# A four-layer convolution network: columns of the last 3x3 convolution transformed too for three of six rows, its result added to the output by an accumulating DMA, squares on ScalarE

## The chip, the cores and the metric

The kernel runs on one core of a Trainium2 chip. The metric is the device time of one execution in microseconds. The kernel before was run three times: median 2744.98 us, lowest 2739.24, highest 2749.27. One more execution was recorded by the hardware profiler; its own time is 2735.2 us and its span, from the first recorded instruction to the last, 2733.4 us.

Names of engines: TensorE (PE, with PEld for its weight loads), VectorE (DVE), ScalarE (ACT), GpSimd (POOL) and SyncE (SP). In this kernel SP issues most loads, ScalarE some stores, and GpSimd some loads and stores.

## The reference, cut to what matters

The input x is [4, 256, 64, 64] in float32. Four layers each add a function of the group norm of x to x:

```
def _gn(v, G=32, eps=1e-5):          # mean and variance over 8 channels x 64 x 64
    ...
    return ((g - m) / jnp.sqrt(s + eps)).reshape(v.shape)

x = x + _L0_conv_ref(_gn(x), ...)    # axial attention along rows, three batch norms
x = x + _L1_conv_ref(_gn(x), ...)    # 3x3 convolution with ternary weights
x = x + _L2_conv_ref(_gn(x), ...)    # two grouped 3x3 convolutions of signs, three batch norms
x = x + _L3_conv_ref(_gn(x), ...)    # 3x3 convolution with generated weights
```

The last layer's 256 x 256 x 3 x 3 weights are generated from a 64 x 64 x 3 x 3 tensor and sixteen pairs (a, b), and the convolution is an ordinary one with a border of zeros and a bias:

```
act = w * a / (1.0 + jnp.exp(w * b))
W = act.transpose(0, 2, 1, 3, 4, 5).reshape(R0 * OOC, R1 * OIC, K1, K2)
out = jax.lax.conv_general_dilated(x, W, window_strides=(1, 1), padding=[(1, 1), (1, 1)], ...)
return out + bias[None, :, None, None]
```

## The kernel before, in words

**The whole.** The layers run one after the other. Between them tensors lie in DRAM scratch: the second layer's sum in x2_d, the third layer's two result parts in z_d and y_d (y_d before its batch norm), the last layer's transformed weights in u3_d. The last layer's input is built when it is read: x2 plus z times a scale per channel, and for the first of two channel tiles also y times sy2.

**The generated weights.** During the first layer's scoring loop, weight_steps (L598) is a generator: each step of the loop calls next(weights) once (L652), so a bit of weight work on VectorE is put between the attention's operations. weights_3(t, dx) makes the six transformed weight rows of one input tile t and one column tap dx and GpSimd's queue stores them; weights_2 follows for the third layer.

**The last convolution.** Channels are two tiles of 128 partitions, t for input and co for output. An image b is cut into halves h of 32 rows. A chunk (b, h, co) is 128 output channels of half an image; there are sixteen. The convolution is a Winograd F(4,3) along rows only: from each group of six input rows, input_rows (L1036) forms six transformed rows k, with 12 VectorE operations of 128x528 for a half of one tile; output_rows (L1055) multiplies each k with its weights and combines six products to four output rows. Columns are handled directly with three taps dx. So a chunk takes 6 rows x 3 taps x 2 input tiles = 36 matmuls of 512 columns (8 row groups by 64) in f32, and every f32 matmul stands in the trace as two records. Products go to a ring of seven PSUM tiles. The combination is one ScalarE copy for each of two products (L1084), 10 VectorE operations (L1086 to L1099), and 4 more (L1101) that add the result to the residual, which is still in SBUF in the half-image buffer xs. GpSimd then stores that half image (finish_3, L1760, sixteen stores of 1 MB).

**Loading an image.** load_3 (L1724) is called for a tile t: SP loads the two halves of x2 (1 MB each) and then z and y in parts of 256 KB through four small buffers; VectorE adds z (L1736) and, for t = 0, y (L1743, L1746). Statistics for the group norm are bn_stats on VectorE (L1114), except for tile 0 of image 0, where the sum comes with the addition (accum_out) and the squares are summed on ScalarE (L1749). norm combines the partitions with small matmuls (L115, L125, L126), and transform has ScalarE write the normalised half into a padded buffer (L1182, L1186) before input_rows.

**The order.** conv_layer (L1120) returns functions, called at L1762 to L1779. rest() writes chunk (b, 0, 0), then the load of the next image's tile 0, chunk (b, 0, 1), the load of tile 1 and its norm, chunk (b, 1, 0), the transforms of the next image's first half, chunk (b, 1, 1), and those of its second half. A scheduler then fixes each engine's order from this text; parts under tc.high_priority are put as early as their data allow. In the order before, image 0's tile 1 is loaded, normalised and transformed under high priority between the last chunks of the third layer. Its first chunk multiplies with tile 1 first (order (1, 0)), since tile 0 needs y_d, which is stored last. Every engine's own queue is in order: an instruction that waits holds those behind it.

**Buffers.** Six half-image buffers x0 to x5 rotate by X_PLACES over the four images, six transformed buffers t0 to t5 over the half images. The small load buffers come in two pairs. The two weight buffers u0 and u1 are loaded by GpSimd's queue (six loads of 768 KB) during the third layer.

Of the kernel before, what the change touches and what calls it, by code (L numbers as in the profile page):

```python
# [41 lines left out]
def network(ctx: ExitStack, tc, x, wqkv, relm, relt, relw, relv, counts, masks, vecs, rowv, ab, w1, l2w1, l2w2, l3w, mats, out):  # L42
# [25 lines left out]
    u3_d = scratch("u3_d", [P, 2, 3, 6, C])  # L68
    bk_d = [dram.tile([P, 2, 3, 4 * 3 * 64], BF16, name=f"bk_d{i}", tag=f"bk_d{i}") for i in range(2)]
# [340 lines left out]
    with ExitStack() as ph:  # L410
# [157 lines left out]

        def weights_2(i, g):
# [28 lines left out]
        def weight_steps():  # L598
            for t in range(2):
                for dx in range(3):  # L600
                    yield from weights_3(t, dx)
                    yield
            for i in range(2):
                for g in range(2):
                    yield from weights_2(i, g)
                    yield
# [137 lines left out]
    def from_scores(general, keep):  # L744
# [291 lines left out]
        def input_rows(v, pad, pinned):  # L1036

            d = [pad[:, r : r + 29 : 4, :] for r in range(6)]
            stt = nc.vector.scalar_tensor_tensor
            start = stt(v[:, 5], d[2], -4.0, d[4], ALU.mult, ALU.add)  # L1040
            if pinned:
                tc.keep_in_program_order(start)
            stt(v[:, 0], d[1], -4.0, d[3], ALU.mult, ALU.add)
            nc.vector.tensor_tensor(v[:, 1], v[:, 5], v[:, 0], ALU.add)  # L1044
            nc.vector.tensor_tensor(v[:, 2], v[:, 5], v[:, 0], ALU.subtract)
            nc.vector.tensor_tensor(v[:, 5], d[4], d[2], ALU.subtract)
            nc.vector.tensor_tensor(v[:, 0], d[3], d[1], ALU.subtract)
            stt(v[:, 3], v[:, 0], 2.0, v[:, 5], ALU.mult, ALU.add)
            stt(v[:, 4], v[:, 0], -2.0, v[:, 5], ALU.mult, ALU.add)
            stt(v[:, 0], d[0], 4.0, d[4], ALU.mult, ALU.add)  # L1050
            stt(v[:, 0], d[2], -5.0, v[:, 0], ALU.mult, ALU.add)
            stt(v[:, 5], d[1], 4.0, d[5], ALU.mult, ALU.add)
            stt(v[:, 5], d[3], -5.0, v[:, 5], ALU.mult, ALU.add)

        def output_rows(ring, taken, op, u, vs, co, xh, bias, name, order):  # L1055


            ms = [None] * 6
            c, sm = [None, None], [None, None]

            def product(k, t, first, last):
                if first:
                    ms[k] = ring[taken[0] % len(ring)].tile([P, 8, 64], F32, name=f"{name}_{k}", tag="conv")
                    taken[0] += 1
                for dx in range(3):
                    nc.tensor.matmul(  # L1066
                        ms[k], lhsT=u[t][:, dx, k, bass.ts(co, P)], rhs=vs[t][:, k, :, dx : dx + 64],
                        start=(first and dx == 0), stop=(last and dx == 2),
                    )

            if order:
                for k in range(6):
                    product(k, order[0], True, False)
            for k in range(6):
                if order:
                    product(k, order[1], False, True)
                else:
                    product(k, 0, True, False)
                    product(k, 1, False, True)
                if k in (2, 4):  # L1080
                    i = k // 2 - 1
                    c[i] = op.tile([P, 8, 64], F32, name=f"{name}_c{i}", tag=f"c{i}", bufs=1)
                    sm[i] = op.tile([P, 8, 64], F32, name=f"{name}_s{i}", tag=f"s{i}", bufs=1)
                    nc.scalar.copy(c[i], ms[k])  # L1084
                    if i == 0:
                        nc.vector.scalar_tensor_tensor(sm[i], ms[1], bias, c[i], ALU.add, ALU.add)  # L1086
                        nc.vector.scalar_tensor_tensor(c[i], ms[1], bias, c[i], ALU.add, ALU.subtract)
                    else:
                        nc.vector.tensor_tensor(sm[i], ms[3], c[i], ALU.add)
                        nc.vector.tensor_tensor(c[i], ms[3], c[i], ALU.subtract)  # L1090
            x4 = xh.rearrange("p (q r w) -> p q r w", r=4, w=64)
            (d12, d34), (s12, s34) = c, sm
            o = [op.tile([P, 8, 64], F32, name=f"{name}_o{r}", tag="o", bufs=1 if general else 2) for r in range(4)]
            nc.vector.tensor_tensor(o[0], ms[0], s12, ALU.add)
            nc.vector.tensor_tensor(o[0], o[0], s34, ALU.add)
            nc.vector.scalar_tensor_tensor(o[1], d34, 2.0, d12, ALU.mult, ALU.add)
            nc.vector.scalar_tensor_tensor(o[2], s34, 4.0, s12, ALU.mult, ALU.add)
            nc.vector.scalar_tensor_tensor(o[3], d34, 8.0, d12, ALU.mult, ALU.add)
            nc.vector.tensor_tensor(o[3], ms[5], o[3], ALU.add)  # L1099
            for r in range(4):  # L1100
                nc.vector.tensor_tensor(x4[:, :, r, :], x4[:, :, r, :], o[r], ALU.add)  # L1101
# [16 lines left out]
        X_PLACES = [(0, 1, 2, 3), (4, 5, 0, 2), (1, 3, 4, 0), (5, 2, 1, 4)]  # L1118

# [777 lines left out]
```

## Time and profile before

| | |
|---|---|
| median of three runs | 2744.98 us |
| the profiled execution, and its span | 2735.2 us, 2733.4 us |
| TensorE busy over the span | 88% |
| VectorE busy over the span | 72% |
| ScalarE busy over the span | 44% |
| last VectorE operation of the third layer's last chunk | about 2193 us |
| first and last matmul of the last convolution | 2192.34 us, 2720.6 us |
| output stores of 1 MB, issue to landing | 4.1 us median |

The profile gives all times in microseconds from the start of the span. A group is named by its line, engine, operation and tiles; its mean is the duration of one instruction, and the idle time is that of its engine just ahead of it, with what ended it. Consecutive VectorE operations overlap a little, so the distance from start to start is shorter than the duration. TensorE's granted clock (PEclk) is given as a share of full speed.

### The profile page before, as it was taken

The page shows a single profiled execution, that of the slowest core. Times are in us where ns is not written, and L with a number is a line of the kernel's source. Part 1 is how long each engine was busy: PE and PEld are TensorE (multiplying, and loading weights), DVE is VectorE, ACT ScalarE, POOL GpSimd, SP SyncE. Part 2 cuts the span into 40 slices and gives each one's busy share as a digit, 9 for nine tenths or more (in the row PEclk, how much of TensorE's full clock was granted, in tenths as well). Part 3 has the DMA queues.
Part 4 walks back from the last instruction along what each step waited for, and adds up shares of the span by engine and source line. Part 5 has one row for each costly group of instructions (what it writes and reads, how often), then busy time and mean ns, then how long its engine had stood idle before and what let it go on. Part 6 is the DMA issues. An engine that isn't in the chain of part 4 may idle for free.

```text
span 2733.4 us, 78106 instructions
## 1 busy us (share of the span) xinstructions
PE 2393.6 (88%) x34632; PEld 1574.3 (58%) x34632; DVE 1978.0 (72%) x3372; ACT 1202.9 (44%) x1984; POOL 105.2 (4%) x201
## 2 busy tenths in 40 slices
PE   7999788889998788888784999998979859999998
PEld 4666555556666566666663777775545424444443
DVE  6665788888675466666567989887888877867742
ACT  3555245555555644454444656553458411110100
POOL 0000100000001000000000000000000000000000
PEclk9999899999999799989986999999989979999999
DMA  6866366667666877777777556424347742424110
GB/s 237 270 199 194 97 182 183 164 169 189 154 150 150 257 258 251 264 241 256 249 240 265 196 173 201 155 101 155 120 157 255 280 155 92 154 93 139 47 45 33
DMA packets 287996, 489.86 MB, mean 179 GB/s; under 512 B 32737, under 2 KB 149089, under 8 KB 274849
## 3 DMA queue, kind: packets, MB, share of 16 engines
q1 hardware_dynamic: 224992, 359.52, 43.3%
q0 software_dynamic: 14400, 66.53, 6.3%
q10 hardware_dynamic: 48256, 58.73, 6.2%
q8 instruction: 273, 4.47, 0.7%
q14 instruction: 75, 0.61, 0.1%
HBM read 281.46 MB, written 203.23 MB: 177 GB/s over the span
## 4 chain that ended last, share of the span: by engine, by line
issue 36%; PE 34%; DVE 13%; DMA 9%; ACT 5%; SPq 2%; POOL 1%; DVEq 0%; POOLq 0%; ACTq 0%
PE dc L1353 10%; PE pd L505 5%; PE po L293 3%; PE pv L308 3%; DMA at_d<-o_False 3%; PE pq L526 3%; PE e_False L867 2%; DMA x<-x_d 2%; DVE pt L877 2%; PE pa_False L945 1%; PE den_False L918 1%; PE pr_False L936 1%; PE pe_False L970 1%; DMA qc_False<-q_d 1%; DVE e_tr L1446 1%
## 5 line engine op out<-in xcount | busy, mean ns | idle before, releaser
L1066 PE MATMUL gc<-gtr,g_u 128*128 128x512 f32 x1152 | 505.3, 601 | 13.3 <-DVE gtr L1044 6.7
L1066 PEld LDWEIGHTS gc<-gtr,g_u 128*128 128x128 f32 x1152 | 219.9, 192 | 289.9 <-issue 271.2
L512 DVE STREAM_TRANSPOSE t<-pd 128x1024 f32<-128x1024 f32 x256 | 304.4, 1228 | 92.3 <-PE pd L505 87.0
L505 PE MATMUL pd<-rm,qb 64*32 64x256 f32 x8192 | 306.1, 389 | 41.4 <-DVE t L512 33.3
L1457 PE MATMUL pc<-e_tr,e_k 128*64 128x512 bf16 x2304 | 265.2, 391 | 20.3 <-DVE e_tr L1446 13.9
L532 ACT ACTIVATE o<-pq 128x512 f32<-128x512 f32 x256 | 150.4, 593 | 267.2 <-PE pq L526 258.4
L1353 PE MATMUL dc<-dh,d_u 128*128 128x512 f32 x768 | 229.7, 410 | 22.5 <-ACT dh L1330 21.4
L505 PEld LDWEIGHTS pd<-rm,qb 64*32 64x32 f32 x8192 | 169.8, 108 | 133.3 <-DVE t L512 58.8
L907 ACT ACTIVATE pt<-pt,sm 128x512 f32<-128x512 f32 x256 | 162.5, 709 | 174.6 <-DVE pt L877 156.4
L1353 PE MATMUL dc<-dl,d_u 128*128 128x512 f32 x768 | 226.6, 405 | 1.9 <-DVE dl L1331 1.8
L1457 PEld LDWEIGHTS <-e_k 128*64 128x64 bf16 x2304 | 147.4, 112 | 135.1 <-issue 28.7
L526 PEld LDWEIGHTS pq<-t,t 64*64 64x64 f32 x8192 | 144.7, 137 | 88.6 <-issue 71.3
L526 PE MATMUL pq<-t,t 64*64 64x64 f32 x8192 | 166.6, 225 | 31.5 <-issue 26.1
L1353 PEld LDWEIGHTS dc<-dh,d_u 128*128 128x128 f32 x768 | 146.3, 192 | 63.4 <-ACT dh L1330 22.9
L877 DVE TENSOR_TENSOR pt<-e_False,si_False 128x1024 f32<-128x1024 f32 x128 | 151.5, 1215 | 31.9 <-PE e_False L867 26.8
L1084 ACT COPY gc_c<-gc 128x512 f32<-128x512 f32 x32 | 18.6, 580 | 345.5 <-PE gc L1066 345.5
L1353 PEld LDWEIGHTS dc<-dl,d_u 128*128 128x128 f32 x768 | 144.8, 190 | 43.2 <-DVE dl L1331 4.7
L867 PE MATMUL e_False<-qc_False,rw 32*128 32x256 f32 x1024 | 130.7, 476 | 26.5 <-DVE pt L877 13.6
L538 ACT ACTIVATE sq<-o 128x1024 bf16<-128x1024 f32 x128 | 135.3, 1057 | 4.0
L293 PE MATMUL po<-xg,wt 128*128 128x512 f32 x256 | 122.3, 618 | 5.9 <-DVE st L300 4.3
L970 PE MATMUL pe_False<-pt,ve 128*32 128x64 f32 x4096 | 92.6, 246 | 38.2 <-issue 30.7
L308 PE MATMUL pv<-wt,xg 128*128 128x256 f32 x512 | 120.2, 383 | 0.0
(401 smaller groups left out, 3594.6 us busy)
## 6 DMA issues: line engine op xcount, KB each, us to landing
si_False<-qk_d SPq DMA_DIRECT2D x64, 1024.0 KB
qk_d<-o SPq DMA_DIRECT2D x496, 128.0 KB
x<-x_d SPq DMA_DIRECT2D x32, 1056.0 KB
xa<-in_x SPq DMA_DIRECT2D x16, 1024.0 KB
vt_d<-vs ACTq DMA_DIRECT2D x32, 512.0 KB
q_d<-qs SPq DMA_DIRECT2D x64, 256.0 KB
qb<-q_d SPq DMA_DIRECT2D x128, 128.0 KB
qc_False<-q_d SPq DMA_DIRECT2D x64, 256.0 KB
```

The source lines that it names most:

```text
L293: nc.tensor.matmul(psf, lhsT=wt[:, t, bass.ts(o, P)], rhs=xg[:, t, :], start=(t == 0), stop=(t == 1))
L308: nc.tensor.matmul(pv[:, j, :], lhsT=xg[:, t, pix], rhs=wt[:, t, C : 2 * C], start=(t == 0), stop=(t == 1),)
L505: nc.tensor.matmul(pds[t][32 * c : 32 * c + 32, m].rearrange("p j k -> p (j k)"), lhsT=q[rows, 2 * (gp % 2) + g, a, 32 * nb : 32 * nb + 32 ...
L512: nc.vector.transpose(ts[t][:, :, 32 * jh : 32 * jh + 32].rearrange("p a j b -> p j a b"), pds[t].rearrange("p m j k -> p j m k"),)
L526: nc.tensor.matmul(ps[nb][64 * g : 64 * g + 64, m, :], lhsT=ts[1][rows, n // 2, :, n % 2], rhs=ts[0][rows, n // 2, :, n % 2], start=True, ...
L532: nc.scalar.activation(o[:, :, n : n + 8, :], ps[nb].rearrange("p n (a b) -> p a n b", b=2), AF.Copy, accum_out=acc[:, nb, gp, col : col + 1],
L867: nc.tensor.matmul(es[x_ // 2][:, x_ % 2, :, :, par], lhsT=rw[rows, 63 - i : 127 - i].rearrange("p j r -> p (j r)"), rhs=q[rows, :, par, k ...
L877: nc.vector.tensor_tensor(dst, e, src, ALU.add)
L907: nc.scalar.activation(s, s, AF.Exp, scale=s2q[:, gp : gp + 1])
L1066: nc.tensor.matmul(ms[k], lhsT=u[t][:, dx, k, bass.ts(co, P)], rhs=vs[t][:, k, :, dx : dx + 64], start=(first and dx == 0), stop=(last and ...
L1353: nc.tensor.matmul(at[k], lhsT=u[t][:, dx, k, bass.ts(co, P)], rhs=v[:, k, :, dx : dx + 64], start=(first and p_ == 0 and dx == 0), stop=( ...
L1457: nc.tensor.matmul(m[64 * g : 64 * g + 64], lhsT=parts[:, g, i, k, dx, :], rhs=vs[g][:, k, 8 * (q % 2) : 8 * (q % 2) + 8, dx : dx + 64], s ...
```

## The change

Of the six transformed rows, k = 0, 2 and 4 are now transformed along columns as well, by a Winograd F(2,3): two output columns from four input columns with four products instead of six. input_rows writes these three rows to a scratch tile (gtm), and a new function input_columns makes four column terms c from it, with four VectorE operations of 768 elements. The rows k = 1, 3, 5 keep the three taps. Weights for the column terms 1 and 2 are prepared by a new part of the weight generator, weights_c, and stored in uc_d; terms 0 and 3 use u3_d with dx = 0 and dx = 2.

output_rows now has nine products per chunk: for each even k two that hold two column terms of 256 columns each (terms 1 and 2, terms 0 and 3), for each odd k one of 512. That is 24 matmuls of 256 columns and 18 of 512. columns and whole combine a pair: two ScalarE operations of 256 and two VectorE operations of 512 for an even row. The result goes to one tile of four rows, o4, with a single buffer.

The residual is no longer added in SBUF for 14 of the 16 chunks. load_3 has ScalarE's queue store the built half image to out as soon as it is complete, and the chunk's result is added onto it by a DMA with accum_op on GpSimd's queue. The last two chunks (b = 3, h = 1) add the residual in SBUF and are stored by SP in halves.

All bn_stats are gone: sums come with the additions, squares are summed on ScalarE. There are four half-image buffers and four transformed buffers, and three small load buffers that z and y share and that ScalarE's square frees. Image 0's y is loaded whole (2 MB) into the buffer of u0, so the u0 weights are loaded after its last reader. Each u takes six loads. In the changed program's order, image 0's additions, norms and transforms all stand after the third layer's last VectorE operation, and its group-norm matmuls after the third layer's matmuls. The first chunk starts seven of nine products with tile 1.

The diff, cut to its core:

```diff
+        def weights_c(t):
...
+            nc.gpsimd.dma_start(out=a, in_=u3_d[:, t, 0, 0:6:2])
+            nc.gpsimd.dma_start(out=c, in_=u3_d[:, t, 2, 0:6:2])
+            nc.gpsimd.dma_start(out=u[:, 3:6], in_=u3_d[:, t, 1, 0:6:2])
+            for _ in range(3):
+                yield
+            v = nc.vector
+            pinned(v.tensor_tensor(c, a, c, ALU.add))
+            v.tensor_scalar(c, c, 0.5, None, ALU.mult)
+            yield
+            pinned(v.scalar_tensor_tensor(u[:, 0:3], u[:, 3:6], 0.5, c, ALU.mult, ALU.add))
+            v.scalar_tensor_tensor(u[:, 3:6], u[:, 3:6], -0.5, c, ALU.mult, ALU.add)
+            nc.gpsimd.dma_start(out=uc_d[:, t].rearrange("p c k o -> p (c k) o"), in_=u)
...
+        def input_columns(w, v):
+
+            f = v.rearrange("p k q w -> p (k q) w")
+            d = [f[:, :, r : r + 63 : 2] for r in range(4)]
+            for c, (i, j, op) in enumerate(
+                ((0, 2, ALU.subtract), (1, 2, ALU.add), (2, 1, ALU.subtract), (3, 1, ALU.subtract))
+            ):
+                nc.vector.tensor_tensor(w[:, c].rearrange("p k q w -> p (k q) w"), d[i], d[j], op)
+
+        TILES = [(0, (1, 2)), (0, (0, 3)), (1, None), (2, (1, 2)), (2, (0, 3)), (3, None), (4, (1, 2)), (4, (0, 3)), (5, None)]
...
+                else:
+                    m = ms[i].rearrange("p q (a w) -> p (q a w)", a=2).rearrange("p (a n) -> p a n", a=2)
+                    for a, c in enumerate(cs):
+                        nc.tensor.matmul(
+                            m[:, a], lhsT=u2[:, c, k // 2, bass.ts(co, P)],
+                            rhs=v2[:, c, k // 2].rearrange("p q w -> p (q w)"), start=first and a == 0, stop=last and a == 1,
+                        )
...
+            def columns(i, copied, scratch_):
+                pair = halves(flat(ms[i]))
+                c2 = halves(copied)
+                nc.scalar.copy(c2[:, 0], pair[:, 1])
+                nc.scalar.mul(c2[:, 1], pair[:, 1], -1.0)
+                sd = halves(scratch_)
+                nc.vector.tensor_tensor(sd, pair[:, 0:1].to_broadcast([P, 2, 256]), c2, ALU.add)
+                return sd
+
+            def whole(i, sd, dst):
+                nc.vector.tensor_tensor(
+                    dst.rearrange("p (n a) -> p a n", a=2), halves(flat(ms[i])), sd, ALU.add
+                )
+
+            o4 = op.tile([P, 8, 4, 64], F32, name=f"{name}_o", tag="o4")
...
-            for r in range(4):
-                nc.vector.tensor_tensor(x4[:, :, r, :], x4[:, :, r, :], o[r], ALU.add)
+            nc.vector.tensor_tensor(o4[:, :, 3, :], ms[8], as_rows(c0), ALU.add)
+            of = o4.rearrange("p q r w -> p (q r w)")
+            if res is None:
+                nc.gpsimd.dma_start(out=out_, in_=of, accum_op=ALU.add)
+            else:
+                for half in range(2):
+                    cols = bass.ts(half, HW // 4)
+                    nc.vector.tensor_tensor(of[:, cols], of[:, cols], res[:, cols], ALU.add)
+                    nc.sync.dma_start(out=out_[:, cols], in_=of[:, cols])
...
+            y0 = ps_["u0"].tile([P, HW], F32, name=f"{name}_y0", tag="u")
+            nc.sync.dma_start(out=y0, in_=y_d[0])
...
+                input_rows([(v1 if k % 2 else m)[:, k // 2] for k in range(6)], pads[h], pinned)
+                input_columns(v2, m)
...
+                        a = ap_.tile([P, HW // 8], F32, name=f"x3_{b}_{t}_{k}", tag="a")
                         nc.sync.dma_start(out=a, in_=z_d[b][bass.ts(t, P), part])
+                        kw = {"accum_out": st[:, k, 0:1]} if t == 1 else {}
                         nc.vector.scalar_tensor_tensor(
+                            xt[:, cols], a, sg[:, t, 0, b : b + 1], xt[:, cols], ALU.mult, ALU.add, **kw
                         )
...
+                        nc.scalar.activation(a, xt[:, cols], AF.Square, accum_out=st[:, k, 1:2])
+                    if b < B - 1 or half == 0:
+                        nc.scalar.dma_start(out=out[b, bass.ts(t, P), bass.ts(half, HW // 2)], in_=xt)
...
             with tc.high_priority():
                 norm(0, slice(1, 2))
                 transform(0, 1, 0)
+            prepare(0, 0)
             load_weights(0, nc.gpsimd)
-            prepare(0, 0)
             norm(0, slice(0, 1))
             transform(0, 0, 0)
```

## The prediction

> **What bounds the kernel now.** I first placed the stage: the last convolution's matmuls are line L1066, and the costliest-groups table of the page gives them the top row.
>
> ```profile
> L1066 PE MATMUL gc<-gtr,g_u 128*128 128x512 f32 x1152 | 505.3, 601 | 13.3 <-DVE gtr L1044 6.7
> ```
>
> 1152 records (two per matmul) take 505.3 us and have 13.3 us of idle time before them. Next, busy times in stretches of 100 us (columns: length, then PE, PEld, DVE, ACT, POOL busy with instruction counts, granted PE clock, DMA share, GB/s):
>
> ```profile
> 2200.00:2300.00 100.00, 78.04 (x173) 34.31 (x172) 69.84 (x145) 13.24 (x25) 1.07 (x2) 0.86 0.42 142
> 2300.00:2400.00 100.00, 100.00 (x239) 44.37 (x238) 84.76 (x151) 13.90 (x16) 1.59 (x3) 1.00 0.37 126
> 2400.00:2500.00 100.00, 100.00 (x239) 44.48 (x238) 79.06 (x141) 13.90 (x16) 1.59 (x3) 1.00 0.34 115
> 2500.00:2600.00 100.00, 100.00 (x238) 44.33 (x237) 67.74 (x123) 13.32 (x15) 1.59 (x3) 1.00 0.17 64
> 2600.00:2700.00 100.00, 100.00 (x235) 44.04 (x234) 33.99 (x53) 3.51 (x6) 2.13 (x4) 1.00 0.10 42
> ```
>
> From 2300 to 2700 TensorE never rests and has its full clock. VectorE follows at 85% where the next image is loaded and transformed, and falls to 34% for the last image. So TensorE sets the pace, with little VectorE room behind it. Waits in 2192 to 2734 (what waits, for what, us, times, longest) agree:
>
> ```profile
> ACT gc_c L1084 <- PE gc L1066: 345.5, 26, 20.0
> DVE gx L1736 <- DMA gx<-x_d: 57.2, 8, 9.6
> PE pst L115 <- DVE sm L1160: 15.3, 1, 15.3
> PE gc L1066 <- DVE gtr L1044: 6.7, 1, 6.7
> ```
>
> The others wait for the matmuls; TensorE waits only at the start. The timeline of PE there (start, length, group, idle before):
>
> ```profile
> 2171.39 0.58 PE L115 MATMUL pst<-sm,mt 128*128 128x1 f32 x2 [6.76 <-DVE sm L1160]
> ...
> 2192.34 15.10 PE L1066 MATMUL gc<-gtr,g_u 128*128 128x512 f32 x28 [6.59 <-DVE pc_o L1469]
> 2222.72 0.59 PE L115 MATMUL pst<-sm,mt 128*128 128x1 f32 x2 [15.28 <-DVE sm L1160]
> ...
> 2236.73 13.80 PE L1066 MATMUL gc<-gtr,g_u 128*128 128x512 f32 x25 [6.67 <-DVE gtr L1044]
> ```
>
> Image 0 is loaded and normalised around the end of the third layer. The first line is the norm of its second channel tile, standing in the third layer's TensorE queue and holding it 6.76 us. From 2236.73 PE runs through to 2720.6. The timeline of the tail:
>
> ```profile
> 2720.00 0.68 DVE L1097 SCALAR_TENSOR_TENSOR gc_o<-gc_s,gc_s 128x512 f32<-128x512 f32 x1
> 2720.60 0.68 DVE L1098 SCALAR_TENSOR_TENSOR gc_o<-gc_c,gc_c 128x512 f32<-128x512 f32 x1
> 2721.20 0.68 DVE L1101 TENSOR_TENSOR gx<-gx,gc_o 128x512 f32<-128x512 f32 x1
> ...
> 2726.14 0.54 POOL L1760 DMA_DIRECT2D out<-gx  x1 [32.99 <-DVEq L1784]
> ```
>
> It shows the price unit for VectorE: an operation of 512 lasts 0.68 us, but the next starts 0.60 later. I use such spacings: 0.60 for 512, 0.66 with a per-partition scalar (lasts 0.74), 0.62 for 528 (lasts 0.70).
>
> [...] The trace has 958 (weight preparation, L595), so the new column operations are priced, about 0.88 us apart. [...] The trace of before has no accumulating DMA.
>
> **The change, part by part.** All sums are against the profiled execution (2735.2 us, span 2733.4); the median of the runs is 2744.98, 9.8 more, added at the end.
>
> *TensorE.* A chunk had 36 matmuls of 512 columns, two records each; in the tail's timeline fourteen records span 6.17 us of which the last takes 0.6, so 0.43 apart (0.4287 over longer runs): 36×2×0.4287 = 30.87 us, an image 123.5. Now 18 remain and 24 have 256 columns. The first layer's 256-column matmuls (L308) run 16 records in 3.45 us, 0.2156 each, their 0.19 us weight loads still hidden. A chunk costs 18×2×0.4287 + 24×2×0.2156 = 25.78 us, an image 103.1, sixteen chunks 412 instead of 494: −81 us if nothing else binds.
>
> *VectorE, per image.* Before: four transforms 4×12×0.62 = 29.8; four chunk outputs 4×(12×0.60+2×0.66) = 34.1; loads 24×0.66 + 16 bn_stats×0.60 = 25.4; small things 3: 92. After: transforms 4×(12×0.62+4×0.88) = 43.8; outputs, with six new column operations and four residual additions less, 4×(14×0.60+2×0.66) = 38.9; loads 24×0.66 + 16 accumulator reads×0.08 = 17.1; 3: 103. So VectorE needs what TensorE needs. The work isn't evenly laid: the last chunk of an image carries the next image's transforms. Seven PSUM tiles against nine per chunk let TensorE run little ahead, and the norm (small VectorE, PE and ScalarE steps, then a 2.10 us pad on ScalarE) leaves VectorE about 7 us with little to do. I take 112 us for a period with a following image (ends: 103, PE alone; 125, VectorE 103 plus 22 of load waits), 108 for the last image.
>
> *ScalarE.* 64 squares of 0.63+0.19 and six 256-column copies (about 0.33) per chunk: 52+32 us over 490, against 14% busy before. Not a bound, but the squares free the load buffers.
>
> *Loads.* Three buffers for all 256 KB parts, each freed by ScalarE's square; a load takes 2.2 to 3 us to arrive (issue 2215.07, use 2218.06). SP's queue is in order, so a late square holds the parts behind it, and VectorE, in order too, then holds the chunk outputs queued behind the addition. 24 parts per image in threes, about 3.8 us a round, is 30 us in 103: hidden if issued early, up to 22 if VectorE waits for most. The transform buffers fall from six to four, so the next image's second-half transforms wait for the last chunk's matmuls.
>
> *Start.* No part of image 0 now stands inside the third layer: its TensorE loses the 6.8 us wait, its VectorE one 7.4 us transform. I put its last VectorE operation near 2180 instead of 2193.5. After it: 8+16 additions gated by loads and squares (25 us), transform of tile 1 (11), norm, transform of tile 0 (19): continuous PE from 2235 with 13 us of work done, where before 2236.73 had 15.4 done. Gain and loss cancel. The u weights (12 loads, half waiting for the y image that borrows their buffer) arrive in that time; they took 14.4 us to land before. Image 0 needs 90 us more, plus 17 for its remaining transforms and image 1's loads on VectorE: image 1 starts at 2342.
>
> *Residual.* Fourteen plain 1 MB stores from ScalarE's queue and fourteen accumulating ones replace sixteen stores. Traffic is cheap here (DMA share 0.37 at most). A plain store lands 4.1 us after issue[...]. The output tile has one buffer, first rewritten about 19 us later, so I cost it at nothing; beyond 19 each us delays fourteen chunks. Below nothing is excluded, as nobody waited for these stores but the end.
>
> *Tail.* The last two chunks are added in SBUF and stored in halves by SP: 9 us from last matmul to end instead of 12.8.
>
> *Weight preparation.* Two steps of four 768-element operations in the first layer's VectorE work: 0 to 7 us, I take 3.
>
> Sum: 2342 + 112 + 112 + 108 = 2674; +9 = 2683; +3 = 2686 span, 2688 execution, −47; with 9.8, **2698 us**.
>
> **Rivals.** *A. VectorE keeps up.* Periods fall to 103 to 106: −20 to −38 more, 2660 to 2678. For: its mean was only 68 to 85%. Against: 103 of work in 103.
>
> *B. VectorE and its loads become the bound.* Periods stay near 125: 2688+3×13 = 2727, median 2737; hardly a gain. For: the 57.2 us of load waits, three buffers. Against: those waits came while VectorE had nothing else to do.
>
> *C. The accumulating DMA holds the output tile: slower.* If 1 MB takes A us, a chunk period is A+7 instead of 27.5. Slower than before from 14×(A−20.5) > 47, A about 24, six times the plain store. At A = 28: 2698+105 = 2803. For: no trace of it. [...]
>
> That the change doesn't shorten TensorE's work is excluded by its counts.
>
> **How the numbers follow.** Chances: forecast 0.52 (own range 2680 to 2720), A 0.16, B 0.20, C 0.12. What a measurement can tell from no change is 0.3%, 8 us: 2737 to 2753. B lies across its lower edge (half faster, a third same, the rest slower), C beyond its upper one: faster 0.79, same 0.06, slower 0.15. The range leaves out C, and the low end of A: 2660 to 2748.
>
> **What would show it.** Right: 1536 matmul records spaced 0.43 and 0.22; PE 88 to 95% busy in the middle, VectorE over 90%; continuous PE from about 2235; accumulating stores landing within 12 us; ScalarE under 30%. PE at 100% means A; VectorE idle on loads or squares with PE under 85% means B; VectorE waiting for an out DMA before writing its output tile means C. A start after 2250, or 256-column records over 0.25 us, would make the sum wrong.

## The result, and the profile after

| | before | after |
|---|---|---|
| median of seven runs | 2744.98 us | 2730.61 us |
| lowest, highest | 2736.14, 2750.61 us | 2722.72, 2742.22 us |
| ratio, after to before | | 0.9952, 95% interval 0.9934 to 0.997 |
| profiled execution, span | 2735.2, 2733.4 us | 2729.02, 2727.2 us |

The changed kernel is faster by about 14 us, 0.5%. The forecast was 47 us. The last convolution's matmuls are two groups now (costliest groups of the kernel after: line, engine, operation, tiles, shape and count; busy time and mean ns; idle before and its releaser):

```profile
L1101 PE MATMUL gc<-gtr,g_u 128*128 128x512 f32 x576 | 261.4, 601 | 2.4 <-DVE gc_c L1160 2.1
L1108 PE MATMUL gc<-gtc,g_u 128*128 128x256 f32 x768 | 186.0, 394 | 27.8 <-issue 15.8
```

Together 447.4 us busy instead of 505.3. The busy times in stretches of 100 us, kernel after, columns as before:

```profile
2200.00:2300.00 100.00, 64.88 (x197) 40.76 (x198) 81.05 (x161) 24.21 (x52) 5.25 (x7) 0.78 0.55 187
2300.00:2400.00 100.00, 86.33 (x270) 51.69 (x268) 85.87 (x163) 23.55 (x49) 2.54 (x3) 0.93 0.50 145
2400.00:2500.00 100.00, 85.15 (x272) 53.32 (x273) 78.52 (x161) 25.38 (x59) 2.52 (x3) 0.93 0.54 158
2500.00:2600.00 100.00, 83.52 (x267) 50.50 (x266) 78.75 (x161) 26.53 (x61) 3.39 (x4) 0.93 0.51 140
2600.00:2700.00 100.00, 98.27 (x317) 59.52 (x316) 78.70 (x118) 10.82 (x25) 2.54 (x3) 1.00 0.21 43
```

Where TensorE never rested before, it now rests 14 to 16% of the time, at a lower mean granted clock (0.93 against 1.00). VectorE isn't at its limit either, at 79 to 86%. So neither engine is the bound; both wait. The waits of the kernel after, in 2160 to 2728:

```profile
PE pst L116 <- DVE sm L1242: 67.5, 4, 29.0
DVE gx L1814 <- DMA x<-z_d: 57.9, 23, 7.9
PE gc L1108 <- issue: 15.8, 1, 15.8
PE gc L1108 <- DVE gc_s L1128: 8.3, 4, 3.1
```

TensorE waits ahead of the small matmuls of a group norm (pst), 29.0 us of it before image 0 begins, and VectorE waits for the 256 KB parts of z. The timeline of PE in the kernel after shows where:

```profile
2230.66 2.90 PE L1108 MATMUL gc<-gtc,g_u 128*128 128x256 f32 x6 [15.76 <-issue]
...
2334.69 0.59 PE L116 MATMUL pst<-sm,mt 128*128 128x2 f32 x2 [11.90 <-DVE sm L1242]
2335.14 2.05 PE L1108 MATMUL gc<-gtc,g_u 128*128 128x256 f32 x4
...
2458.80 0.59 PE L116 MATMUL pst<-sm,mt 128*128 128x2 f32 x2 [12.05 <-DVE sm L1242]
...
2581.01 0.59 PE L116 MATMUL pst<-sm,mt 128*128 128x2 f32 x2 [14.57 <-DVE sm L1242]
```

Three times the norm matmul of the next image stands in TensorE's queue, around the end of chunk (b, 1, 0), and its statistics aren't there: 11.9, 12.1 and 14.6 us. The four records right after the first of these waits start 0.43 us apart (the second 0.57 after the first), at a granted clock of 0.50; at full clock they start 0.22 apart. One late load, with what lies around it (timeline of all engines, kernel after):

```profile
2408.47 0.84 POOL L1172 DMA_DIRECT2D out<-gc_o  x1 [30.87 <-DVE gc_o L1169]
...
2410.88 0.32 SPq L1812 DMA_DIRECT2D x<-z_d  x1
...
2414.53 0.34 ACTq L1829 DMA_DIRECT2D out<-gx  x1
...
2415.22 0.32 SPq L1812 DMA_DIRECT2D x<-z_d  x1
...
2420.45 0.75 DVE L1814 SCALAR_TENSOR_TENSOR gx<-x,sg,gx 128x512 f32<-128x512 f32 x1 [5.39 <-DMA x<-z_d]
2421.12 0.74 DVE L1160 SCALAR_TENSOR_TENSOR gc_c<-gc,bias,gc_c 128x512 f32<-128x512 f32 x1
```

GpSimd issues an accumulating store, which lands 10.8 us later, at 2419.26. SP issues a part of z 2.4 us after it. VectorE can use that part only at 2420.45, 9.6 us after its issue, and the chunk's own output operation (L1160) has stood behind that addition. By the order of issues and uses the part issued at 2415.22, after the residual's store and as soon as a buffer was free, is the next one and is used at 2423.61. Then all three buffers are taken, and SP issues nothing more until 2421.23.

All six waits of over 4 us after 2240 are of this kind. Each part was issued 0.6 to 2.4 us after the start of an accumulating store and took 7.6 to 10.9 us, and five of the six came 0.2 to 1.5 us after that store had landed. Two parts issued 0.7 us after a store of the residual, with no accumulating store under way, took 5.0 us. Of the 124 us from 2335 to 2459 VectorE is busy for 102.7 and, in about that stretch (2330 to 2460), waits 15.6 us for such parts.

### The profile page after: what moved, and what is told of

Its sections match the earlier page's. It is cut to its first block, busy times and chain, and to the rows that moved or that the text cites. A ratio compares the mean times of both kernels' runs of the same rounds, so it can differ in the third digit from the quotient of the medians.

```text
span 2727.2 us, 78998 instructions
## 1 busy us (share of the span) xinstructions
PE 2319.7 (85%) x34824; PEld 1613.4 (59%) x34824; DVE 2036.8 (75%) x3508; ACT 1254.4 (46%) x2160; POOL 119.9 (4%) x213
## 5 line engine op out<-in xcount | busy, mean ns | idle before, releaser
L506 PE MATMUL pd<-rm,qb 64*32 64x256 f32 x8192 | 310.9, 390 | 49.7 <-DVE t L513 35.8
L1534 PE MATMUL pc<-e_tr,e_k 128*64 128x512 bf16 x2304 | 258.5, 386 | 20.5 <-DVE e_tr L1523 11.3
L1101 PE MATMUL gc<-gtr,g_u 128*128 128x512 f32 x576 | 261.4, 601 | 2.4 <-DVE gc_c L1160 2.1
L1108 PE MATMUL gc<-gtc,g_u 128*128 128x256 f32 x768 | 186.0, 394 | 27.8 <-issue 15.8
L1108 PEld LDWEIGHTS gc<-gtc,g_u 128*128 128x128 f32 x768 | 149.6, 197 | 73.8 <-issue 42.1
L1101 PEld LDWEIGHTS gc<-gtr,g_u 128*128 128x128 f32 x576 | 109.8, 192 | 119.7 <-issue 112.1
```

Source lines behind the costliest of these rows:

```text
L506: nc.tensor.matmul(pds[t][32 * c : 32 * c + 32, m].rearrange("p j k -> p (j k)"), lhsT=q[rows, 2 * (gp % 2) + g, a, 32 * nb : 32 * nb + 32 ...
L1101: nc.tensor.matmul(ms[i], lhsT=u1[:, dx, k // 2, bass.ts(co, P)], rhs=v1[:, k // 2, :, dx : dx + 64], start=(first and dx == 0), stop=(las ...
L1108: nc.tensor.matmul(m[:, a], lhsT=u2[:, c, k // 2, bass.ts(co, P)], rhs=v2[:, c, k // 2].rearrange("p q w -> p (q w)"), start=first and a = ...
L1534: nc.tensor.matmul(m[64 * g : 64 * g + 64], lhsT=parts[:, g, i, k, dx, :], rhs=vs[g][:, k, 8 * (q % 2) : 8 * (q % 2) + 8, dx : dx + 64], s ...
```

## The experiments

Every run was compared with the kernel before on the same chip. Medians of the kernel before differ a little between chips (2737 to 2745), so ratios are compared; "gain" is the ratio's distance from the changed kernel's 0.9952, times 2740 us. By the intervals of the two ratios a gain is uncertain by about 7 to 13 us. The last four columns come from the timeline of PE in each kernel's one profiled execution, by counting columns of matmuls: where image 0 ends, and how long images 1, 2 and 3 take. The end of image 0 carries the scatter of the layers before: over the changed kernel and its variants the third layer's last VectorE operation comes between 2176.7 and 2191.8.

| kernel | ratio to before (95%) | gain over the change | image 0 ends | 1 | 2 | 3 |
|---|---|---|---|---|---|---|
| before | 1 | -13 us | 2348.6 | 124.3 | 124.3 | 123.6 |
| the change | 0.9952 (0.9934 to 0.997) | | 2363.5 | 125.2 | 123.4 | 105.6 |
| eight buffers | 0.9834 (0.9813 to 0.9855) | 32 | 2357.9 | 110.0 | 111.7 | 103.2 |
| five buffers | 0.9872 (0.9835 to 0.9908) | 22 | 2360.8 | 110.8 | 122.4 | 103.2 |
| no early residual stores | 0.9893 (0.9863 to 0.9923) | 16 | 2366.7 | 119.4 | 117.6 | 103.2 |
| plain store, no accumulate | 0.9871 (0.9827 to 0.9914) | 22 | 2359.3 | 116.7 | 118.6 | 105.6 |
| square into its own tile | 0.9975 (0.9958 to 0.9992) | -6 | 2366.2 | 125.2 | 129.9 | 103.2 |
| six buffers | 0.9894 (0.9853 to 0.9935) | 16 | 2353.2 | 119.9 | 118.3 | 103.2 |
| six buffers, stores late | 0.9914 (0.9893 to 0.9935) | 10 | 2355.1 | 125.3 | 122.4 | 103.2 |
| taps for all rows | 1.007 (1.0043 to 1.0097) | -32 | 2373.5 | 124.3 | 124.3 | 123.6 |
| fourteen buffers | 0.9814 (0.9791 to 0.9837) | 38 | 2360.2 | 109.7 | 111.2 | 103.2 |
| eight buffers, plain store | 0.9778 (0.9753 to 0.9803) | 48 | 2356.7 | 107.1 | 105.1 | 103.2 |
| eight buffers, no column operations | 0.9732 (0.9708 to 0.9757) | 60 | 2348.4 | 103.9 | 103.9 | 103.2 |
| fourteen buffers, image 0 too | 0.9821 (0.979 to 0.9852) | 36 | 2351.3 | 109.5 | 111.1 | 103.2 |

In most of these kernels more changes than the text of the edit says. The scheduler orders the queues anew when buffers or stores change: in the changed kernel the additions of the next image stand singly or in twos between the chunk's operations, with eight buffers ten to thirteen stand in a row. Only the plain stores leave the order of the last convolution on VectorE, ScalarE and SP as it was. What the other kernels gain is therefore the effect of the edit together with its new order; the two were not told apart.

### How many parts can be under way

The first theory was the loads' round trip; its rivals were crowded DMA engines and VectorE's own work. Eight buffers, with room made by overlapping weight slots, so that some weights are overwritten by others:

```diff
-            ps_ = {k: pool(ph, f"{name}_{k}", 3 if k == "a" else 1) for k in layout.split()}
+            ps_ = {k: pool(ph, f"{name}_{k}", 8 if k == "a" else 1) for k in layout.split()}
...
-                u = ps_[f"u{t}"].tile([P, 21, C], F32, name=f"{name}_u{t}", tag="u")
+                u = ps_[f"u{t}"].tile([P, 16, C], F32, name=f"{name}_u{t}", tag="u")
...
-                u1 = u[:, 12:21].rearrange("p (d k) o -> p d k o", d=3)
+                u1 = u[:, 7:16].rearrange("p (d k) o -> p d k o", d=3)
```

> The changed kernel with eight instead of three load buffers for the 256 KB parts of z and y. Room for them comes from letting five of the 21 weight slots of each u tile overlap others, so the weights are wrong; their matmuls are the same in number and size. Theory 1 (the loads' round trip: a part can be asked for only when ScalarE's square or VectorE has emptied one of three buffers, so the norm of the next image comes late and its small matmuls, standing in TensorE's queue, hold TensorE about 12 us per image): TensorE's wait for the norm falls from 11.9, 12.0 and 14.6 us to under 4 each, the last matmul comes 30 to 45 us earlier, time 30 to 45 us less than the changed kernel. Theory 2 (residual stores and accumulating DMAs crowd the DMA engines, the number of buffers is secondary): loads still arrive late, 5 to 15 us less. Theory 3 (VectorE's 103 us of work per image set the period): VectorE stays as busy per image and the period falls by less than 8 us, 0 to 15 us less in all.

Measured: 2692.24 us, 32 us less by the ratios. Waits of the eight-buffer kernel in 2160 to 2740, and its busy times over images 1 and 2:

```profile
PE gc L1108 <- DVE gc_s L1128: 20.3, 3, 11.9
DVE gx L1823 <- DMA yq<-y_d: 17.2, 3, 5.9
DVE gx L1814 <- DMA x<-z_d: 9.7, 11, 3.0
```

```profile
2358.00:2468.00 110.00, 106.02 (x344) 65.15 (x343) 102.01 (x196) 28.95 (x65) 3.36 (x4) 0.98 0.57 172
2468.00:2579.00 111.00, 106.54 (x342) 65.57 (x341) 98.87 (x191) 28.48 (x65) 3.39 (x4) 0.97 0.41 112
```

VectorE's waits for parts fall from 63.0 us (57.9 for z, 5.1 for y) to 26.9, TensorE's waits for the norms of images 1 to 3 are gone, and the periods are 110 and 112 us, the 112 of the forecast. VectorE is 93 and 89% busy. The first theory's numbers come out, with its new order as said above; the third falls, since the same VectorE work fits into 12 to 15 us less. Of the waits that are left in images 1 and 2, one per image is long (5.5 and 5.9 us), again for a part issued 1.0 us after the start of an accumulating store. With five buffers (same edit, two slots overlapping):

> As with eight buffers, but with five (two of 21 weight slots overlap). Theory 1: most of the gain of eight buffers, 20 to 40 us less than the changed kernel, since two more parts can be under way while one of 2.3 to 5.4 us arrives. Theory 2: 3 to 10 us less. Theory 3: 0 to 10 us less.

2703.32 us, 22 us of gain: inside the first theory's range. In the profiled execution image 1 gets the short period and image 2 does not, so five look just short of enough.

### Crowding of the DMA engines

The early stores left out:

```diff
-                    if b < B - 1 or half == 0:
-                        nc.scalar.dma_start(out=out[b, bass.ts(t, P), bass.ts(half, HW // 2)], in_=xt)
```

> The changed kernel without ScalarE's early stores of the residual (fourteen of 1 MB), so the output lacks the residual for those half images. Theory 1: the two loads per image of 5 us fall to 2.3, which gives 3 times 6 us, 12 to 20 us less than the changed kernel; TensorE's waits for the norm fall by about 5 us each but stay. Theory 2: the waits of VectorE for parts (57.9 us in all) mostly vanish, 30 to 45 us less. Theory 3: 0 to 8 us less.

2711.66 us, a gain of 16: the first theory's range, not the second's. VectorE's waits for parts of z fall to 36.3 us. The norms of images 1 to 3 hold TensorE for 35.8 us, against 38.5; the 5 us less for each that were expected did not come. Six waits of 4.3 to 6.0 us are left, and all six are for parts issued beside an accumulating store: the residual's stores alone are not what makes them late. Next the accumulate as a plain store; the order of instructions in the last convolution is unchanged:

```diff
-                nc.gpsimd.dma_start(out=out_, in_=of, accum_op=ALU.add)
+                nc.gpsimd.dma_start(out=out_, in_=of)
```

> The changed kernel with the accumulating DMA replaced by a plain store on the same queue, so the residual is overwritten. Theories 1 and 3: nobody waits for the accumulate, its landing falls from 9.1 to about 4 us, and the time changes by less than 6 us. Theory 2: [...] loads arrive earlier, 6 to 20 us less. If the accumulating DMA itself held the output tile, 20 us or more less.

2708.68 us, a gain of 22: the first theory's "less than 6" was wrong, and the second was nearer. DMA issues in 2160 to 2728 (last: median us to landing), the kernel after, then this one:

```profile
out<-gc_o POOLq DMA_DIRECT2D x14, 1024.0 KB, 9.1
```

```profile
out<-gc_o POOLq DMA_DIRECT2D x14, 1024.0 KB, 4.8
```

The size touches the last case named, an output tile held by the accumulate, but neither kernel's waits have VectorE waiting for that tile. What the accumulating store costs is the lateness of the parts issued beside it: these are the waits of the kernel with plain stores in 2160 to 2728, the first with 28.5 us ahead of image 0:

```profile
PE pst L116 <- DVE sm L1242: 51.4, 4, 28.5
DVE gx L1814 <- DMA x<-z_d: 37.5, 22, 5.3
```

VectorE's waits for z fall from 57.9 to 37.5 us, the longest after 2240 is 3.1 instead of 7.9, and the norms of images 1 to 3 hold TensorE for 22.9 us instead of 38.5. As the order is the same, this is the cleanest of the experiments: the late parts cost the time. Do enough buffers hide that? The same edit in the eight-buffer kernel:

> The eight-buffer kernel with a plain store in place of the accumulating DMA (weights and output wrong as said for the two). With three buffers the plain store gained 22 us. If crowding acts only by lengthening the loads' round trip, eight buffers hide it and the plain store gains under 5 us here. If the accumulate also costs in another way, it gains 10 us or more again.

They don't altogether: 2681.38 us, 15 us less than with eight buffers and the accumulate by the ratios (about 9 either way), 10.7 by the two profiled executions. The periods fall from 110.0 and 111.7 to 107.1 and 105.1. The difference lies in the chunk during which the next image is loaded: 31.7 and 33.6 us with the accumulate, 26.7 and 26.8 without; the chunk after it gives 2.2 us of this back in image 1. VectorE's waits for parts in images 1 and 2 fall from 12.2 to 5.9 us. The expected "under 5 us" was wrong; the accumulate still costs with eight buffers.

### Which part of the round trip

The square writes its unused result onto the load buffer and so keeps it. Given a tile of its own, it frees the buffer earlier:

```diff
-                        nc.scalar.activation(a, xt[:, cols], AF.Square, accum_out=st[:, k, 1:2])
+                        junk = ap_.tile([P, HW // 8], BF16, name=f"sq_{b}_{t}_{k}", tag="junk", bufs=1)
+                        nc.scalar.activation(junk, xt[:, cols], AF.Square, accum_out=st[:, k, 1:2])
```

> The changed kernel with ScalarE's square writing to a bf16 tile of its own instead of onto the load buffer, so that a buffer is free when VectorE's addition has read it; still three buffers. If it is the square that makes the round trip long (theory 1a), every round gets about 0.9 us shorter and the time is 10 to 20 us less than the changed kernel (2730.6). If it is that only three parts can be under way while one arrives (theory 1b), 0 to 8 us less, and TensorE's waits for the norm stay above 8 us per image.

2735.33 us, no gain. So the 0.9 us that the square adds to a round by the estimate (0.63 us, and 0.19 for reading its sum, in the trace of the changed kernel) isn't what counts, and the waits for the norms of images 1 to 3 stay above 8 us each, as the second reading has it. Then a kernel that keeps all weights, with six buffers, three of them in gtm, the scratch tile of the row transform:

```diff
+                more = mp.tile([P, 3, 8, 66], F32, name=f"x3m_{b}_{t}", tag="tm") if b > 0 else None
+
+                def buffer(name):
+                    slot = taken[0] % 6
+                    taken[0] += 1
+                    if more is None or slot < 3:
+                        return ap_.tile([P, HW // 8], F32, name=name, tag="a")
+                    return more.rearrange("p k q w -> p (k q w)")[:, bass.ts(slot - 3, HW // 8)]
```

> A whole kernel with right weights: square onto its own tile, and for images 1 to 3 six load buffers, the three added ones lying in the scratch tile of the row transform, which is idle while an image is loaded. Theory 1b: the waits for the norm of images 1 to 3 nearly vanish, periods of 108 to 114 us, 25 to 40 us less than the changed kernel, near 2698. Theory 2 (crowded DMA engines): 5 to 15 us less. Theory 3 (VectorE's work): 0 to 10 us less.

2714.22 us, a gain of 16, less than expected. The norms' waits are gone, but another wait took their place. The timelines of VectorE and of PE in this kernel:

```profile
2396.67 0.74 DVE L1824 SCALAR_TENSOR_TENSOR gx<-x,sg,gx 128x512 f32<-128x512 f32 x1
2405.60 0.75 DVE L1824 SCALAR_TENSOR_TENSOR gx<-x3m,sg,gx 128x512 f32<-128x512 f32 x1 [8.18 <-DMA x3m<-z_d]
...
2410.22 0.68 DVE L1128 TENSOR_TENSOR gc_s<-gc,gc_o 128x512 f32<-128x512 f32 x1
```

```profile
2410.95 3.78 PE L1108 MATMUL gc<-gtc,g_u 128*128 128x256 f32 x8 [12.98 <-DVE gc_s L1128]
```

VectorE sits in an addition that waits for a part (issued 0.4 us after the start of an accumulating store); the chunk's first output operation (L1128) stands behind it and five more additions; the PSUM tiles stay full and TensorE stops for 13 us. So a late part has two ways to TensorE: through the norm, or through the outputs behind a waiting addition. Moving the residual stores behind the norm:

```diff
-                    if b < B - 1 or half == 0:
-                        nc.scalar.dma_start(out=out[b, bass.ts(t, P), bass.ts(half, HW // 2)], in_=xt)
...
                     norms[b, t] = nb, rs[:, i : i + 1]
+                    for half in range(2):
+                        if b < B - 1 or half == 0:
+                            tc.keep_in_program_order(
+                                nc.scalar.dma_start(out=out[b, bass.ts(t, P), bass.ts(half, HW // 2)], in_=xs[b, t][half])
+                            )
```

> As with six buffers, and the early stores of the residual moved behind the norm of their image, when no part of an image is being loaded. Theory 1b: with six buffers the crowding is hidden already, within 5 us of the six-buffer kernel. Theory 2: a further 8 to 20 us less.

2715.2 us, the same within what these runs can tell. With that place of the stores nothing is seen to be won.

### What the change is worth without its matmul saving

```diff
-        TILES = [(0, (1, 2)), (0, (0, 3)), (1, None), (2, (1, 2)), (2, (0, 3)), (3, None), (4, (1, 2)), (4, (0, 3)), (5, None)]
+        TILES = [(k, None) for k in range(6)]
...
-                input_rows([(v1 if k % 2 else m)[:, k // 2] for k in range(6)], pads[h], pinned)
-                input_columns(v2, m)
-                vs[b, t, h] = v1, v2
+                input_rows([v1[:, k] for k in range(6)], pads[h], pinned)
+                vs[b, t, h] = v1, None
```

> One half of the change undone: the columns are handled by three taps for all six rows again (36 matmuls of 512 per chunk), with the residual stored early and added by the accumulating DMA, squares on ScalarE, three load buffers. Forecast's reading (TensorE then needs 123.5 us per image, more than VectorE's 74 and the loads' 110 to 115): TensorE runs without rest in the middle and the time is within 12 us of the kernel before. If the residual stores and squares slow the middle by themselves, 20 us or more above the kernel before.

2756.91 us: 16 us above the kernel before by the medians, 19 by the ratio (12 to 27). That is more than the 12 that I gave, and the interval takes in the rival's 20; but the rival put the loss in the middle, and it isn't there. Timeline of PE of this kernel, and VectorE's waits for z in it from 2312 on:

```profile
2309.03 0.59 PE L116 MATMUL pst<-sm,mt 128*128 128x2 f32 x2 [8.93 <-DVE sm L1233]
...
2312.04 123.27 PE L1101 MATMUL gc<-gtr,g_u 128*128 128x512 f32 x282
...
2437.45 122.13 PE L1101 MATMUL gc<-gtr,g_u 128*128 128x512 f32 x284
...
2561.72 183.93 PE L1101 MATMUL gc<-gtr,g_u 128*128 128x512 f32 x428
```

```profile
DVE gx L1802 <- DMA x<-z_d: 22.6, 9, 7.8
```

Loads are late here too (with y, 33 us of waits from 2312 on, against 41 in the changed kernel), but under 124 us of matmuls per image TensorE runs without rest. This kernel also has less VectorE work, 74.7 us in image 1 against 103.7, so it doesn't tell whether the longer matmuls alone would hide the waits. The loss is nearly all in image 0, which ends 24.9 us later than before; the middle is not slowed, image for image. So the column transform is worth some 32 us in the changed kernel, and the rest of the change costs 19.

### A kernel without the load waits, and what bounds it

The two padded tiles are idle while an image is loaded, too. With them and gtm there are fourteen buffers; the borders are set to zero again before the next transform:

```diff
+                    if slot < 7:
+                        return flat[0][:, bass.ts(slot - 3, HW // 8)]
+                    if slot < 10:
+                        return more.rearrange("p k q w -> p (k q w)")[:, bass.ts(slot - 7, HW // 8)]
+                    return flat[1][:, bass.ts(slot - 10, HW // 8)]
...
+                if b > 0 and t == 0:
+                    set_up(h)
                 nb, rs = norms[b, t]
```

> A whole kernel with right weights: square onto its own tile, and for images 1 to 3 fourteen load buffers, three in the pool, three in the row scratch tile and eight in the two padded tiles, which are idle while an image is loaded and get their zero borders again before the next transform. If the loads' round trip is what the forecast missed, VectorE's waits for parts of images 1 to 3 fall from some 16 us to under 5 per image and the time is 30 to 45 us less than the changed kernel (2730.6), near or below the eight-buffer kernel (2692). If six buffers already gave all there is to get by buffers, it stays near 2714.

2689.53 us, ratio 0.9814 to the kernel before: 38 us better than the changed kernel, with all weights and the accumulate in place, and so better than both. In images 1 and 2 VectorE no longer waits for any part, where under 5 us per image were expected. Its busy times over images 1, 2 and 3:

```profile
2360.00:2470.00 110.00, 106.06 (x345) 65.65 (x344) 102.14 (x203) 28.69 (x65) 3.36 (x4) 0.98 0.58 173
2470.00:2581.00 111.00, 107.08 (x343) 65.87 (x342) 104.90 (x207) 28.92 (x65) 3.39 (x4) 0.97 0.43 119
2581.00:2684.00 103.00, 103.00 (x337) 63.41 (x335) 68.30 (x103) 10.47 (x26) 2.54 (x3) 1.00 0.20 42
```

VectorE is now busy for 93 to 95% of images 1 and 2. To see whether it holds the remaining 7 us above TensorE's 103, the column operations were left out of the eight-buffer kernel:

```diff
-                v2 = ps_[f"t{2 * h + t}"].tile([P, 4, 3, 8, 32], F32, name=f"{name}tc_{b}_{t}_{h}", tag="tc")
+                v2 = v2s[t, h]
...
-                input_columns(v2, m)
```

where v2s holds four tiles that are set to zero once.

> The eight-buffer kernel without the 64 column operations of the input (14 us of VectorE per image); the 256-column matmuls read tiles that hold zeros, so the result is wrong. If VectorE is the second bound, as the forecast has it (103 us of work per image, periods of 110), the periods of images 1 and 2 fall to TensorE's 103 and the time is 20 to 35 us less than with eight buffers. If TensorE alone sets the pace there, under 10 us less.

2669.35 us, 28 us less than with eight buffers, in the first reading's range; the periods are 103.9 and 103.9. But 9.5 us of it lie in image 0, whose first matmul comes at 2181.2 instead of 2220.3: the edit also takes away what the 256-column matmuls waited for. Its busy times:

```profile
2350.00:2453.00 103.00, 103.00 (x339) 63.59 (x338) 95.40 (x200) 31.60 (x75) 3.36 (x4) 1.00 0.70 217
2453.00:2556.00 103.00, 103.00 (x339) 63.61 (x339) 78.95 (x150) 23.39 (x49) 3.39 (x4) 1.00 0.32 72
```

TensorE without a gap. So in the fourteen-buffer kernel VectorE and TensorE nearly share the bound. That VectorE's amount of work sets the last 6 to 8 us is not shown, though: with eight buffers it is busy for 201.6 us over images 1 and 2 with either kind of store, and the periods are 110.0 and 111.7 or 107.1 and 105.1. With fourteen buffers TensorE waits 3.9 us at 2408.88 for a chunk's first output operation, which stands behind twelve additions in a row; another order was not tried. Last, more buffers for image 0 and its y behind tile 1's parts:

```diff
-                    slot = count[0] % 14
+                    slot = count[0] % (14 if b > 0 else 7)
...
+            load_y0()
             prepare(0, 0)
```

> As with fourteen buffers, and for image 0 seven (three of the pool, four in the second padded tile), with the 2 MB load of its y behind the parts of tile 1 on SP's queue. If image 0's late start comes from the same round trip of loads, the norm of its tile 1 comes some 10 us earlier (2211.6 with fourteen buffers) and the time is 5 to 15 us less than with fourteen buffers (2689.5). If the start hangs on memory that the third layer frees late or on VectorE's work, under 4 us less.

The norm of tile 1 does come 14.6 us earlier, but in these two profiled executions the third layer had also ended 7.7 us earlier, 5.3 of them already gained by 1900; and the time, 2687.85 us, can't be told from 2689.53. Timeline of PE in this kernel:

```profile
2196.97 0.58 PE L116 MATMUL pst<-sm,mt 128*128 128x1 f32 x2 [17.81 <-DVE sm L1244]
...
2239.44 6.04 PE L1101 MATMUL gc<-gtr,g_u 128*128 128x512 f32 x10 [9.02 <-DMA g_u<-u_d]
```

TensorE starts earlier and then waits 9.0 us for the weights of tile 0, which can be loaded only when y has left their buffer. In the profiles the last matmul still comes 9 us sooner, and most of that is the same 7.7; in the timed runs that does not show.

## Why the prediction was wrong, by its own steps

The sign was right; the size was not, and the chosen case was not the one that came. By the profiled executions the last matmul came at 2717.8 instead of 2674, 43.8 us late: image 0 21.5, image 1 13.2, image 2 11.5, image 3 2.4 early.

- **TensorE's step held.** From the first start to the start of what follows, sixteen 256-column records at full clock take 3.45 us and twelve 512-column ones 5.15, the prices used. The 1536 records named among the signs were a slip: 16 chunks of 36 and 48 records are 1344, and 576 + 768 are in the trace. The last image, without a follower, takes 105.6 us (forecast 108), and 103.2 where nothing disturbs it.
- **VectorE's step held in its amount.** 103 us of work per image were forecast; 102.7 are busy in 124. The price of the new column operations rests on the trace of before alone, where a VectorE tensor_tensor of 768 elements lasts 958 ns (L595, median of 8), and it holds: in the kernel after they last 957 ns (L1084, median of 64), and four in a row take 3.56 us. The period of 112 does come with eight buffers, but partly by luck: the sum had put the 9 us above 103 down to uneven work and the norm, while one wait of 5.5 to 5.9 us beside an accumulating store is in each, and plain stores bring the periods to 107.1 and 105.1.
- **The loads' step failed.** It had worked out 30 us of rounds in 103 and up to 22 of waits, and called them "hidden if issued early", at 2.2 to 3 us for a load. That price was taken where no accumulating store was under way. The six waits of over 4 us were for loads beside one, which took 7.6 to 10.9 us, and with three buffers SP could not issue the next ones meanwhile. So rival B came, with its period of 125 (measured 125.2 and 123.4), at a chance of 0.20. The argument against B looked at other waits: the 57.2 us of before are for the 1 MB halves of x2, those of after for the 256 KB parts.
- **The residual's step failed with it.** That an accumulating store lands within 12 us, well before its output tile is rewritten, was my estimate; no trace of before showed such a store. It took 9.1 us, against 4.8 for the plain store in its place and 4.1 in the kernel before; the tile never waited, rival C did not come. But "I cost it at nothing" was wrong: the plain store, with the order unchanged, is 22 us faster with three buffers and 15 with eight. I had looked at the mean DMA share, 0.37, where the latency of single 256 KB loads mattered. So two terms failed together, the price of a load and the cost of the accumulating store, and mending either takes most of it away: eight and fourteen buffers give 32 and 38 us, where 33 were missing by the medians. That these agree is partly luck. With fourteen buffers images 1 to 3 take 324 us where the sum had 332, while image 0 still ends 18 us late.
- **The start's step failed in part.** The third layer's last VectorE operation comes at 2182.8 (forecast 2180). But 13 us of first products were to be done by 2235; only about 2 were, as the first came at 2230.66. The stretch of the 24 additions ahead of the first transform, costed at 25 us, took 38 (2182.8 to 2220.8): 4 us of a batch norm's small operations that the sum had left out, then 34 with some 15 of waits for parts of z. No accumulating store was under way yet; the longest wait, 5.9 us, is for a part that took 9.4 beside a store of the residual and two 1 MB loads. From 2235 to the end of image 0 there were 27 us of waiting and slow clock instead of 17, the norm of image 1 with 11.9 the largest. "Gain and loss cancel" was wrong: in the kernel with taps, which keeps the matmuls of before, image 0 ends 24.9 us later.
- **The tail** took 9.4 us (forecast 9), and weight preparation isn't seen to cost more than the 3 us allowed: the first layer's scoring takes 577 to 589 us in the thirteen kernels that have it, 578 in the one without. ScalarE stayed at 24 to 27%; a pair of its 256-column copies takes 0.66 us in the kernel after (2405.20 to 2405.86), the 0.33 each of the sum. None of these mattered.
- **The signs named in advance** pointed to B, but not sharply: PE under 85% with VectorE idle on loads was its mark, 88 to 95% that of the forecast; PE measured 83.5 to 86.3% in the middle, 85.0 on average, and VectorE did wait for loads.

What stays open: image 0, the largest single part of the miss with 21.5 us; how the 15 us of the accumulate with eight buffers divide between later parts and anything else; how much of what more buffers gain is due to the new order; and what image 0 could gain if y had room of its own.

## What to carry to other kernels

When a change takes work from the engine that hid everything else, price each wait that was hidden, not by its share but by how many transfers can be under way at once: latency divided by buffers, against the time between uses. Take the latency beside the transfers that the change itself adds, not from a profile without them (here 7.6 to 10.9 us instead of 2.2 to 3). A wait in an engine's queue also held what stood behind it, so a late load stopped the matmuls through the norm (11.9 to 14.6 us in the changed kernel) or through the outputs (13.0 us with six buffers), and mending one way showed the other. Tiles that idle during a load (scratch, padded inputs) can be lent to it.

## What the runs showed of the hardware that was not expected

An accumulating 1 MB DMA landed 9.1 us after issue (median of 14), a plain one from the same tile 4.8. Though no engine waited for it, replacing it shortened the kernel by 22 us, and the six 256 KB loads that VectorE waited for longest after 2240 (4.1 to 7.9 us) had been issued 0.6 to 2.4 us after the start of one and came 7.6 to 10.9 us after their own issue, mostly just after it had landed, against 5.0 beside a plain store of the residual and 2.2 to 3 in the kernel before. It isn't the accumulation alone: at the start of the stage one such load took 9.4 us beside a store of the residual and two 1 MB loads. After 12 us without a large matmul, the granted clock was 0.50 and TensorE's next records started 0.43 us apart instead of 0.22, so there a gap cost more than its length.
